# Where attention's sums are divided by their denominators

## The chip, the cores and the metric

The kernel runs on one core of a Trainium2 chip. The metric is the device time of one launch in microseconds, as the median of several runs; before the change it is 3389.54 us over 3 runs. Engines are named as in the profile: PE is TensorE, DVE is VectorE, ACT is ScalarE, POOL is GpSimd, and SP is the queue that issues the DMAs.

## The reference

Two layers of graph attention and one transformer layer work on 4096 rows of 256 features, all under the same 4096 x 4096 mask. Only the transformer layer is touched by the change:

```
qkv = layer_norm(x, g1, be1) @ w_qkv            # 8 heads of 32
scores = einsum('nhd,mhd->hnm', q, k) * SCALE
attn = softmax(where(mask, scores, -inf))
out = einsum('hnm,mhd->nhd', attn, v).reshape(n, 256)
x = x + out @ w_proj + b_proj
ff = gelu(layer_norm(x, g2, be2) @ w1 + b1) @ w2 + b2
return x + ff
```

The softmax is computed as exponentials without a shift, then sums of values (numerators) and sums of weights (denominators), and one multiplication by the inverse denominator per row and head.

## The kernel before

The transformer layer is `unshifted_transformer`. It has three parts: queries, keys and values; attention; and a last stage with the output projection, a layer norm and the two matmuls of the feed-forward part. Rows are taken in 8 blocks (`nb`) of 512. The 256 features are two groups (`c`) of 128, each holding four heads, so that attention consists of 16 such quads of heads, `(nb, c)`, with 32 tiles of 128 keys (`mt`) in each. A unit is one `(nb, c, mt)`; there are 512.

For every unit PE computes the scores of four heads in two halves (L1652), ACT takes the exponentials in place in PSUM (L1659), and DVE multiplies by the mask and writes `u_e` to SBUF (L1661). PE adds values weighted by `u_e` to `u_av` (L1666, from `weigh`). For the denominators, POOL adds the `u_e` of two neighbouring units (`u_both`, L1749), and PE multiplies these sums by ones and accumulates `u_dn` (L1666, from `total`), so that POOL has two additions for every pair of units. `u_e` has 10 buffers, `u_both` 6, scores 3 and each of the two sums one bank of PSUM. The order of PE, ACT and DVE in attention is that of the program text (`manual_schedule`); that of POOL and SP, and that of all engines in the last stage, is a planner's, which puts an instruction where it expects it to be ready.

At the end of a quad, ACT copies the numerators from PSUM to `u_num` (L1682, two buffers) and the denominators to `u_den` (L1697). The denominators' way to their inverse goes through DRAM. Four DMAs store one row per head to `den_d` (L1699). Then a list of later steps, `later`, gives one step after every second unit: `step_load` loads them as 128 x 16 (L1702), `step_invert` takes the reciprocal on DVE and stores it to `inv_d` (L1706, L1707), `step_spread` loads it with each head's row repeated over 32 partitions into `u_wide` by four DMAs (L1712), and `step_out` multiplies `u_num` by `u_wide` on DVE (L1720) and stores the product to `att_d` in DRAM (L1721). The steps of the last quad run after the last unit.

The last stage starts with `rows_of(0)`, which loads the residual rows `u_xres` (L742 in the profile) and `u_att`, 128 x 2 x 512, from `att_d` (L1786), each with two buffers. `projected` adds the bias to the residual rows on POOL (L1793), multiplies `u_att` by `w_proj` on PE (L1797), adds the product to the residual rows on DVE (L1804), takes mean, squares and root (L1375, L1383, L1390), normalises (L1401, L1403), and adds the next bias on POOL (L1807). Then PE transposes the normalised rows (L1416), multiplies by `w1` (L1833), ACT takes the gelu (L1840), PE multiplies by `w2` (L1849), DVE adds (L1856) and the rows go out in four DMAs (L1857). The loop over blocks has the loads and `projected` of block `nb + 1` in front of block `nb`'s feed-forward part:

```
for nb in range(NNB):
    more = nb + 1 < NNB
    if more:
        res_next, res_n = projected(*rows_of(nb + 1))
...
    if more:
        hn = turned(res_n)
...
```

Of the kernel before, what the change touches and what calls it, by code (L numbers as in the profile page):

```python
# [8 lines left out]
F32 = mybir.dt.float32  # L9
# [8 lines left out]
ALU = mybir.AluOpType  # L18
# [4 lines left out]
P = 128  # L23
# [694 lines left out]
def spread(src, ap):  # L718

    return bass.AP(tensor=src.tensor, offset=src.offset, ap=ap)  # L720
# [765 lines left out]
def unshifted_transformer(  # L1486
# [22 lines left out]
    nc = tc.nc  # L1509
    N, D = out.shape  # L1510
    DC = D // P
# [3 lines left out]
    NB = 512  # L1515
# [3 lines left out]
    HC = 4  # L1519
    O = P // HC  # L1520
# [7 lines left out]
    inv_d = dram.tile([NQ, HC, NB], F32, name="inv_d")  # L1528
    att_d = dram.tile([DC, P, N], F32, name="att_d")
# [7 lines left out]
    with ExitStack() as scope:  # L1537
# [31 lines left out]
        with ExitStack() as qkv:  # L1569
# [8 lines left out]
            for nb in range(NNB):  # L1578
                cols = slice(nb * NB, (nb + 1) * NB)
# [43 lines left out]
                for b in (nb - 1,) if nb + 1 < NNB else (nb - 1, nb):  # L1623
                    if b >= 0:
                        at = slice(b * NB, (b + 1) * NB)
# [11 lines left out]
        tail = scope.enter_context(tc.tile_pool(name="u_tail", bufs=1))  # L1637
        ps_s = scope.enter_context(tc.tile_pool(name="u_ps_s", bufs=3, space=PSUM))
        ps_a = scope.enter_context(tc.tile_pool(name="u_ps_a", bufs=1, space=PSUM))
        sums_of = {}  # L1640
        later = []
# [32 lines left out]
        def weigh(nb, c, mt, es):  # L1674
            if mt == 0:
                sums_of["av"] = ps_a.tile([P, NB], F32, name="u_av")
            h = c * HC
            lefts = [v_sb[:, mt, (h + j) * O : (h + j + 1) * O] for j in range(HC)]
            four(sums_of["av"], lefts, es, mt == 0, mt == NT - 1)
            if mt == NT - 1:  # L1680
                num = tail.tile([P, NB], F32, name="u_num", bufs=2)
                nc.scalar.copy(num, sums_of["av"])  # L1682
                sums_of[nb, c] = num

        def total(nb, c, mt, both):

# [5 lines left out]

        def quad_end(nb, c):
            at = nb * DC + c
            cols = slice(nb * NB, (nb + 1) * NB)
            den = tail.tile([P, NB], F32, name="u_den")
            nc.scalar.copy(den, sums_of["dn"])  # L1697
            for j in range(HC):
                nc.sync.dma_start(den_d[at, j : j + 1, :], den[j * O : j * O + 1, :])  # L1699

            def step_load():
                nc.sync.dma_start(dens[:, at, :], spread(den_d[at], [[QI, P], [1, QI]]))  # L1702

            def step_invert():
                inv = tail.tile([P, QI], F32, name="u_inv")
                nc.vector.reciprocal(inv, dens[:, at, :])  # L1706
                nc.sync.dma_start(spread(inv_d[at], [[QI, P], [1, QI]]), inv)  # L1707

            def step_spread():
                wide = tail.tile([P, NB], F32, name="u_wide")  # L1710
                for j in range(HC):
                    nc.sync.dma_start(  # L1712
                        wide[j * O : (j + 1) * O, :],
                        spread(inv_d[at, j : j + 1, :], [[0, O], [1, NB]]),
                    )
                sums_of["wide"] = wide

            def step_out():
                num = sums_of.pop((nb, c))
                nc.vector.tensor_tensor(num, num, sums_of["wide"], op=ALU.mult)  # L1720
                nc.sync.dma_start(att_d[c, :, cols], num)  # L1721

            later.extend([step_load, step_invert, step_spread, step_out])

# [6 lines left out]
        for i in range(len(units) + 5):  # L1733
            if i < len(units):
                nb, c, mt = units[i]
# [23 lines left out]
    with ExitStack() as scope:  # L1759
        big = scope.enter_context(tc.tile_pool(name="u_big", bufs=1))  # L1760
        ln = scope.enter_context(tc.tile_pool(name="u_ln2", bufs=2))
        tail = scope.enter_context(tc.tile_pool(name="u_ff", bufs=2))
        ps_m = scope.enter_context(tc.tile_pool(name="u_ps_m", bufs=8, space=PSUM))
        wp_sb = big.tile([P, DC, D], F32, name="u_wp")
        nc.sync.dma_start(wp_sb, w_proj.rearrange("(c p) e -> p c e", p=P))

        def by_row(src, name):
            t = big.tile([P, D], F32, name=name)
            nc.sync.dma_start(t, spread(src, [[0, P], [1, D]]))
            return t.unsqueeze(1).to_broadcast([P, TB, D])  # L1770

        bp_sb = by_row(b_proj, "u_bp")
        wp_sb = big.tile([P, DC, D], F32, name="u_wp")
        nc.sync.dma_start(wp_sb, w_proj.rearrange("(c p) e -> p c e", p=P))


        inside = big.tile(list(dens.shape), F32, name="u_inside")
        nc.vector.tensor_scalar(inside, dens, DEN_MIN, DEN_MAX, op0=ALU.max, op1=ALU.min)
        nc.vector.tensor_tensor(inside, inside, dens, op=ALU.is_equal)
        nc.vector.tensor_reduce(checks.column(), inside, AX.XY, ALU.min)  # L1780

        def rows_of(nb):
            res = tail.tile([P, TB, D], F32, name="u_xres")
            rows.load(res, nb * TB)
            att = tail.tile([P, DC, NB], F32, name="u_att")
            nc.sync.dma_start(  # L1786
                att, att_d[:, :, nb * NB : (nb + 1) * NB].rearrange("c p n -> p c n")
            )
            return res, att

        def projected(res, att):

            nc.gpsimd.tensor_tensor(res, res, bp_sb, op=ALU.add)  # L1793
            for t in range(TB):
                pp = ps_m.tile([P, NB], F32, name="misc")
                for k in range(DC):
                    nc.tensor.matmul(  # L1797
                        pp[:, :D],
                        att[:, k, t * P : (t + 1) * P],
                        wp_sb[:, k, :],  # L1800
                        start=(k == 0),
                        stop=(k == DC - 1),
                    )
                nc.vector.tensor_tensor(res[:, t, :], res[:, t, :], pp[:, :D], op=ALU.add)  # L1804
            res_n = ln.tile([P, TB, D], F32, name="ln_rows")
            norms.normed(res_n, res, *norms.moments(res, ln.tile([P, D], F32, name="ln_square")))
            nc.gpsimd.tensor_tensor(res, res, b2_sb, op=ALU.add)  # L1807
            return res, res_n


        first = rows_of(0)
        b2_sb = by_row(b2, "u_b2")
        w1_sb = big.tile([P, DC, F], F32, name="u_w1")
        nc.sync.dma_start(w1_sb, w1.rearrange("(c p) f -> p c f", p=P))
        w2_sb = big.tile([P, FC, D], F32, name="u_w2")
        nc.sync.dma_start(w2_sb, w2.rearrange("(c p) e -> p c e", p=P))
        def turned(res_n):
            hn = ln.tile([P, DC, NB], F32, name="ln_cols")
            for c in range(DC):
                norms.turned(hn, c, res_n, ps_m.tile([P, NB], F32, name="misc"), 2)  # L1820
            return hn

        res, res_n = projected(*first)
# [5 lines that stand above are left out]
            hid = tail.tile([P, FC, NB], F32, name="u_hid")  # L1829
            for f in range(FC):  # L1830
                ph = ps_m.tile([P, NB], F32, name="misc")
                for k in range(DC):
                    nc.tensor.matmul(  # L1833
                        ph,
                        w1_sb[:, k, f * P : (f + 1) * P],
                        hn[:, k, :],
                        start=(k == 0),
                        stop=(k == DC - 1),
                    )
                nc.scalar.activation(  # L1840
                    hid[:, f, :], ph, AF.Gelu_apprx_tanh, bias=norms.sb["b1"][:, f : f + 1]
                )
            if more:
                hn = turned(res_n)
            for t in range(TB):
                at = t * P
                po = ps_m.tile([P, NB], F32, name="misc")
                for f in range(FC):
                    nc.tensor.matmul(  # L1849
                        po[:, :D],  # L1850
                        hid[:, f, at : at + P],
                        w2_sb[:, f, :],
                        start=(f == 0),
                        stop=(f == FC - 1),
                    )
                nc.vector.tensor_tensor(res[:, t, :], res[:, t, :], po[:, :D], op=ALU.add)  # L1856
                nc.sync.dma_start(  # L1857
                    out[nb * NB + at : nb * NB + at + P, :], res[:, t, :]
                )
            if more:  # L1860
                res = res_next
# [110 lines left out]
```

## Time and profile before

| | |
|---|---|
| median of the runs | 3389.54 us (3386.7 to 3389.91, 3 runs) |
| the profiled execution | 3386.81 us; its span 3385.0 us |
| granted PE clock, mean | 0.982 |
| busy, share of the span | PE 93%, DVE 86%, ACT 78%, POOL 39% |
| 1930 to 3040 us, within attention: busy of 1110 us | DVE 1095.06, POOL 1071.65, PE 1046.26, ACT 917.19 |
| 3110 to 3385 us, last stage: busy of 275 us | PE 258.92, ACT 91.62, DVE 48.67, POOL 35.26 |
| first and last `u_both` start | 1850.3 and 3091.1 us |
| L1720, `u_num` times `u_wide`, 16 times | 691 to 3671 ns, median 3251 |
| L1712, loads of `u_wide`, 64 DMAs of 64 KB | 415 ns of SP each (median) |

The span is the time from the first to the last record of one profiled execution; the launch takes a little longer, and the median of the runs differs a little from this one execution. Busy times count an instruction from its start to its end as the profiler sees them, with any waiting in between. Attention runs from about 1850 to 3094 us, the last stage from there to the end.

### The profile page before, as it was taken

The page shows a single profiled execution, that of the slowest core. Times are in us where ns is not written, and L with a number is a line of the kernel's source. Part 1 is how long each engine was busy: PE and PEld are TensorE (multiplying, and loading weights), DVE is VectorE, ACT ScalarE, POOL GpSimd, SP SyncE. Part 2 cuts the span into 40 slices and gives each one's busy share as a digit, 9 for nine tenths or more (in the row PEclk, how much of TensorE's full clock was granted, in tenths as well). Part 3 has the DMA queues.
Part 4 walks back from the last instruction along what each step waited for, and adds up shares of the span by engine and source line. Part 5 has one row for each costly group of instructions (what it writes and reads, how often), then busy time and mean ns, then how long its engine had stood idle before and what let it go on. Part 6 is the DMA issues. An engine that isn't in the chain of part 4 may idle for free.

```text
span 3385.0 us, 109959 instructions
## 1 busy us (share of the span) xinstructions
PE 3161.2 (93%) x49300; PEld 2316.7 (68%) x49300; DVE 2897.8 (86%) x3242; ACT 2638.5 (78%) x3417; POOL 1326.4 (39%) x600
## 2 busy tenths in 40 slices
PE   4899999999889999999988999999999999997998
PEld 3799999999879999999965433333333333333666
DVE  5899999999889989999975999999999999996111
ACT  4799899898768888888875887888888888875332
POOL 2300000000220000000000999999999999996110
PEclk8999999999999999999999999999999999998999
DMA  6656545531211212111126010101010110002110
GB/s 209 204 180 207 155 152 170 146 91 32 80 56 34 90 52 71 40 59 59 28 73 180 2 49 18 39 21 33 21 32 27 26 45 12 28 11 79 42 45 27
DMA packets 210706, 247.44 MB, mean 73 GB/s; under 512 B 88304, under 2 KB 131568, under 8 KB 210224
## 3 DMA queue, kind: packets, MB, share of 16 engines
q1 hardware_dynamic: 210224, 240.31, 23.7%
q8 instruction: 388, 6.36, 0.8%
q14 instruction: 94, 0.77, 0.1%
HBM read 197.80 MB, written 42.47 MB: 71 GB/s over the span
## 4 chain that ended last, share of the span: by engine, by line
DVE 23%; PE 13%; POOL 7%; issue 5%; ACT 4%; DMA 1%; SPq 0%; DVEq 0%; POOLq 0%; ACTq 0%
DVE u_e L1661 20%; POOL u_both L1749 7%; PE misc L1849 3%; PE bank L1330 2%; PE u_ps L1652 2%; PE misc L1595 2%; PE u_av L1666 2%; ACT u_ps L1659 1%; ACT t L1078 1%; PE misc L1833 1%; PE u_dn L1666 1%; PE misc L1614 1%; PE misc L1416 1%; DVE t L1085 1%; DMA u_xres<-rows 1%
## 5 line engine op out<-in xcount | busy, mean ns | idle before, releaser
L1330 PE MATMUL bank<-vst,t 128*128 128x66 f16 (+1 forms) x24576 | 1523.4, 203 | 53.2 <-DVE t L1085 46.0
L1330 PEld LDWEIGHTS <-t 128*128 128x128 fp8e4 x24576 | 1504.9, 97 | 74.3 <-DVE t L1085 55.7
L1749 POOL TENSOR_TENSOR u_both<-u_e 128x1024 f32<-128x1024 f32 x512 | 1198.1, 2389 | 884.6 <-DMA u_k<-half_d 839.6
L1330 PE MATMUL bank<-vst,mask 128*128 128x132 f16 x8192 | 1505.0, 222 | 1.8 <-issue 1.8
L1078 ACT ACTIVATE t<-s_b,g_terms 128x1024 int8<-128x1024 f32 x1151 | 1248.9, 1173 | 100.7 <-PE bank L1330 93.1
L1661 DVE SCALAR_TENSOR_TENSOR u_e<-u_mask,u_ps 128x1024 f32<-128x1024 uint8 x1024 | 1171.0, 1212 | 15.8 <-ACT u_ps L1659 13.8
L1659 ACT ACTIVATE u_ps<-u_ps 128x1024 f32<-128x1024 f32 x1024 | 1010.6, 1010 | 219.4 <-PE u_ps L1652 180.9
L1330 PEld LDWEIGHTS <-mask 128*128 128x128 fp8e4 x8192 | 803.3, 98 | 0.0
L1652 PE MATMUL u_ps<-u_q,u_k 128*32 128x512 f16 x8192 | 637.2, 384 | 79.5 <-DVE u_e L1661 64.6
L1652 PEld LDWEIGHTS <-u_k 128*32 128x32 f16 x8192 | 279.0, 96 | 618.7 <-issue 566.2
L1085 DVE TENSOR_TENSOR t<-t,mask 128x2048 int32<-128x2048 int32 x256 | 590.9, 2308 | 107.0 <-ACT t L1078 85.7
L1080 DVE TENSOR_SCALAR t<-s_b,g_terms 128x1024 fp8e4<-128x1024 f32 x897 | 634.7, 750 | 0.0
L1666 PE MATMUL u_av<-u_e,u_v 128*32 128x512 f32 x4096 | 545.0, 602 | 0.1
L1019 POOL TENSOR_TENSOR vst<-g_prod,vst 128x528 f16<-128x528 f32 x32 | 39.0, 1232 | 817.8 <-DVE vst L1018 793.7
L1666 PE MATMUL u_dn<-u_both,u_ones 128*32 128x512 f32 x2048 | 271.9, 597 | 1.7 <-POOL u_both L1749 1.7
L1666 PEld LDWEIGHTS u_av<-u_e,u_v 128*32 128x32 f32 x4096 | 136.7, 110 | 95.5 <-issue 3.1
L1840 ACT ACTIVATE u_hid<-misc,n_b 128x512 f32<-128x512 f32 x64 | 42.4, 685 | 142.0 <-PE misc L1833 141.9
L1856 DVE TENSOR_TENSOR u_xres<-u_xres,misc 128x256 f32<-128x256 f32 x32 | 13.5, 421 | 122.7 <-PE misc L1849 122.7
L1849 PE MATMUL misc<-u_w,u_hid 128*128 128x256 f32 x512 | 111.8, 379 | 0.0
L1833 PE MATMUL misc<-ln_cols,u_w 128*128 128x512 f32 x256 | 111.2, 592 | 0.0
L1336 ACT COPY ev_broad<-bank 128x396 f32<-128x396 f32 x192 | 89.7, 476 | 22.4 <-PE bank L1330 19.1
L1849 PEld LDWEIGHTS misc<-u_w,u_hid 128*128 128x128 f32 x512 | 96.7, 190 | 13.3 <-issue 0.5
(145 smaller groups left out, 1656.1 us busy)
## 6 DMA issues: line engine op xcount, KB each, us to landing
g_adj<-in_adj_dram SPq DMA_DIRECT2D x123, 512.0 KB
mask<-mask SPq DMA_DIRECT2D x128, 256.0 KB
s_b<-s_d SPq DMA_DIRECT2D x64, 512.0 KB
u_mask<-mask SPq DMA_DIRECT2D x32, 512.0 KB
mask<-stage SPq DMA_DIRECT2D x48, 256.0 KB
rows<-e_x SPq DMA_DIRECT2D x32, 256.0 KB
half_d<-u_halves SPq DMA_DIRECT2D x32, 256.0 KB
u_q<-half_d SPq DMA_DIRECT2D x32, 256.0 KB
```

Of the source, the lines that this page charges most:

```text
L1078: nc.scalar.activation(to.bitcast(I8), s, AF.Sign, bias=negd, scale=-1.0)
L1080: nc.vector.tensor_scalar(to, s, negd, None, op0=ALU.is_ge, saturate=False)
L1085: nc.vector.tensor_tensor(both, both, m32.unsqueeze(1).to_broadcast(list(both.shape)), op=ALU.bitwise_and)
L1330: nc.tensor.matmul(to, left, right, start=k not in opened, stop=last)
L1336: nc.scalar.copy(ev[0][:, a:b].rearrange("p s v -> p (s v)"), acc[k][:, : (b - a) * 2 * VW],)
L1652: nc.tensor.matmul(ps[r * O : (r + 1) * O, j, :], k_st[:, h, at : at + O], q_st[:, h, :], start=True, stop=True,)
L1659: nc.scalar.activation(ps, ps, AF.Exp, scale=SCALE)
L1661: nc.vector.scalar_tensor_tensor(e, mask, 0.0, ps, op0=ALU.not_equal, op1=ALU.mult)
L1666: nc.tensor.matmul(to[j * O : (j + 1) * O, :], lefts[j], es[j // 2][:, j % 2, :], start=start, stop=stop,)
L1749: nc.gpsimd.tensor_tensor(both, es_of[i - 1][u], es_of[i][u], op=ALU.add)
L1833: nc.tensor.matmul(ph, w1_sb[:, k, f * P : (f + 1) * P], hn[:, k, :], start=(k == 0), stop=(k == DC - 1),)
L1849: nc.tensor.matmul(po[:, :D], hid[:, f, at : at + P], w2_sb[:, f, :], start=(f == 0), stop=(f == FC - 1),)
```

## The change

The numerators leave attention as they are: `weigh` stores `u_num` to `att_d` right after ACT's copy. `quad_end` keeps the steps that load and invert the denominators and store `inv_d`; `step_spread` and `step_out` are gone. In the last stage `rows_of` also loads the inverse denominators of a block, both groups of four heads in one tile `u_wide` of 128 x 2 x 512 with two buffers, by four DMAs, and `projected` multiplies `u_att` by it on DVE before the projection's matmuls.

```diff
@@ weigh
                 num = tail.tile([P, NB], F32, name="u_num", bufs=2)
                 nc.scalar.copy(num, sums_of["av"])
-                sums_of[nb, c] = num
+                nc.sync.dma_start(att_d[c, :, nb * NB : (nb + 1) * NB], num)
@@ quad_end
-            def step_spread():
-                wide = tail.tile([P, NB], F32, name="u_wide")
-                for j in range(HC):
-                    nc.sync.dma_start(
-                        wide[j * O : (j + 1) * O, :],
-                        spread(inv_d[at, j : j + 1, :], [[0, O], [1, NB]]),
-                    )
-                sums_of["wide"] = wide
-
-            def step_out():
-                num = sums_of.pop((nb, c))
-                nc.vector.tensor_tensor(num, num, sums_of["wide"], op=ALU.mult)
-                nc.sync.dma_start(att_d[c, :, cols], num)
-
-            later.extend([step_load, step_invert, step_spread, step_out])
+            later.extend([step_load, step_invert])
@@ rows_of, projected
-            return res, att
-
-        def projected(res, att):
+            inv = tail.tile([P, DC, NB], F32, name="u_wide")
+            for j in range(HC):
+                nc.sync.dma_start(
+                    inv[j * O : (j + 1) * O],
+                    spread(inv_d[nb * DC, j : j + 1, :], [[0, O], [HC * NB, DC], [1, NB]]),
+                )
+            return res, att, inv
+
+        def projected(res, att, inv):
 
             nc.gpsimd.tensor_tensor(res, res, bp_sb, op=ALU.add)
+            nc.vector.tensor_tensor(att, att, inv, op=ALU.mult)
```

## The prediction

> **What bounds the kernel now.** I read the page's groups first, because the change takes one VectorE (DVE) multiplication out of each of the 16 groups of four heads ("quads") of attention. Columns: line, engine, operation, output and inputs, count, then busy us and mean ns of one, then the idle time before it.
>
> ```profile
> L1749 POOL TENSOR_TENSOR u_both<-u_e 128x1024 f32<-128x1024 f32 x512 | 1198.1, 2389 | 884.6 <-DMA u_k<-half_d 839.6
> ...
> L1661 DVE SCALAR_TENSOR_TENSOR u_e<-u_mask,u_ps 128x1024 f32<-128x1024 uint8 x1024 | 1171.0, 1212 | 15.8 <-ACT u_ps L1659 13.8
> L1659 ACT ACTIVATE u_ps<-u_ps 128x1024 f32<-128x1024 f32 x1024 | 1010.6, 1010 | 219.4 <-PE u_ps L1652 180.9
> ```
>
> Attention has 256 pairs of key tiles. A pair is 4 exponentials, 4 maskings and 2 GpSimd (POOL) additions. Next come the instructions of the multiplication's line, with minimum/median/maximum in ns, and the DVE timeline around one of them (start, us, engine, line).
>
> ```profile
> L1720 DVE TENSOR_TENSOR u_num<-u_num,u_wide x16: 691/3251/3671, 1953.0 to 3111.0; 128x512 f32<-128x512 f32 x16
> ...
> 2176.59 9.13 DVE L1661 SCALAR_TENSOR_TENSOR u_e<-u_mask,u_ps 128x1024 f32<-128x1024 uint8 x8
> 2185.64 3.29 DVE L1720 TENSOR_TENSOR u_num<-u_num,u_wide 128x512 f32<-128x512 f32 x1
> 2188.85 5.81 DVE L1661 SCALAR_TENSOR_TENSOR u_e<-u_mask,u_ps 128x1024 f32<-128x1024 uint8 x5
> 2195.85 58.47 DVE L1661 SCALAR_TENSOR_TENSOR u_e<-u_mask,u_ps 128x1024 f32<-128x1024 uint8 x51 [1.18 <-ACT u_ps L1659]
> ```
>
> The same instruction takes 691 ns after attention has ended and about 3250 within it. DVE looks 98.7% busy (1095 of 1110 us from 1930 to 3040), but some 2.5 us of each multiplication are waiting that is counted as busy. So I don't take DVE for the bound, and look at POOL's timeline (brackets: idle before).
>
> ```profile
> 2113.64 74.74 POOL L1749 TENSOR_TENSOR u_both<-u_e 128x1024 f32<-128x1024 f32 x32 [1.76 <-DVE u_e L1661]
> 2190.14 9.38 POOL L1749 TENSOR_TENSOR u_both<-u_e 128x1024 f32<-128x1024 f32 x4 [1.76 <-DVE u_e L1661]
> 2200.79 65.33 POOL L1749 TENSOR_TENSOR u_both<-u_e 128x1024 f32<-128x1024 f32 x28 [1.26 <-DVE u_e L1661]
> ```
>
> POOL runs without a break except after each multiplication: 1.76 us at once, and in 10 of 15 cases 1.26 to 1.49 us more some 12 us later. The view by stage explains the second gap (columns: stretch, length, busy us and count of PE, PEld, DVE, ACT, POOL, granted clock, DMA share, GB/s).
>
> ```profile
> 1879.00:1953.00 74.00, 72.71 (x912) 30.63 (x911) 73.94 (x66) 64.70 (x68) 74.00 (x33) 1.00 0.05 13
> 1953.00:1965.00 12.00, 8.50 (x92) 3.00 (x88) 10.76 (x9) 5.86 (x6) 10.21 (x6) 0.86 0.07 24
> ```
>
> While DVE waits, TensorE (PE) starves, its clock falls, and ACT, DVE and POOL in turn lack work. In the stretch before the first multiplication (the first of the two lines) the clock is whole and POOL is busy for all of 74 us. **POOL is the bound, interrupted by the multiplications.**
>
> **What the Trainium skill says.** "SBUF — State Buffer", Who interferes with whom: a DVE instruction with two SBUF inputs fully blocks against a GpSimd instruction that reads SBUF, while one with at most one SBUF input doesn't contend. The trace agrees: 3251 against 691 ns for L1720 (two SBUF inputs), while u_e, with only the mask in SBUF, keeps its pace beside a busy POOL. "VectorE: DVE Perf Modes", The TRN2 errata: an fp32 tensor_tensor takes (N+151)/0.96 ns; for N=512 that is 691, just the trace's minimum. "Perfetto Trace Analysis", GPSIMD Engine Instruction: time these by start-to-start spacing. Here 28 additions in 65.33 us with the last at 2.389 give (65.33-2.389)/27 = 2.331 us; the mean of 2.389 would be too long. "TensorE: Matmul & The Clock Gate", What's actually happening: the clock is halved after an idle window of about 3.4 us. The trace shows 0.86 over those 12 us, or 1.7 us of clock lost, which is 3.4 us at half.
>
> **The change part by part.**
>
> *Attention, DVE.* 15 multiplications leave, 3.05 to 3.67 us each, 49.3 us in sum (the 16th ran after the last tile). But POOL sets the pace: 2 x 2.331 = 4.66 us a pair, against DVE's 4 x 1.144 = 4.58 (56 maskings in 64.15 us) and ACT's 4 x 1.01 = 4.04. PE's pair, at full clock, lasts 4.53 in the trace with some waiting in it. So not 49 but POOL's idle time is gained: 15 x 1.76 = 26.4, and the ten second gaps, 13.6: **-40.0 us**. Check: a quad lasts (3037.65-1953.04)/14 = 77.47 us now; 32 x 2.331 = 74.6 at POOL's pace; 15 x 2.9 = 43. Next late is POOL's addition; DVE then waits for PE, which waits for POOL's sum. Lower bound of the gain: the first gaps alone, 26; upper: 43.
>
> *Attention, SP.* Per quad 4 loads of u_wide (0.415 us of issue each) leave; the store of att_d moves up some 26 us, to the copy on ACT. SP waits there for ACT and might hold what is queued behind: den_d's stores, which wait for a copy 5 us later anyway, and the mask and query loads of the next block, asked for most of a quad ahead. Nothing, as long as that lead stands; without it, up to those 5 us per quad. No instruction is added to POOL, PE or ACT; num's two buffers come free sooner.
>
> *The start of the last stage.* The first projection waited for u_att; now it waits for four u_wide loads and a multiplication too. Lines of the timelines of SP, PE and DVE:
>
> ```profile
> 3096.90 0.47 SPq L1786 DMA_DIRECT2D u_att<-att_d  x1
> 3101.08 6.00 PE L1797 MATMUL misc<-u_wp,u_att 128*128 128x256 f32 x16 [6.54 <-DMA u_att<-att_d]
> 3107.39 1.72 SPq L1712 DMA_DIRECT2D u_wide<-inv_d  x4
> 3109.15 0.42 SPq L742 DMA_DIRECT2D u_xres<-rows  x1
> ...
> 3113.45 3.39 DVE L1403 TENSOR_SCALAR ln_rows<-u_xres,n_mean,n_dev 128x256 f32<-128x256 f32 x4
> ```
>
> Four issues last 1.7 us, so the last load lands about that much behind u_att; the multiplication of 128x1024 isn't in the trace: (1024+151)/0.96 = 1.22 us by the page above, and 0.42 at 256 and 0.69 at 512 extend to the same. Together +2.9; bounds +1.2 (loads issued early) and +5 (behind POOL's addition of 2.35 too). Against it, SP no longer stands before the last quad's u_wide loads (3107.39) until inv_d has landed, so u_xres of block 1 comes before 3109.15, and POOL's addition for it no longer meets ln_rows, four instructions that last 3.39 us there and 1.38 in later blocks: -1.5. Bounds 0 and -2. Sum **+1.4 us**.
>
> *Each later block.* 4 more DMAs of 128 KB and 1.22 us of DVE. PE is the bound here, 32.8 of 33 us. The loads reach two blocks ahead (u_att at 3154.18 serves the projection at 3217), so neither transfers nor the wait of PE for att matter. SP's four issues, 1.7 us, fit between its waits. What has no slack is the chain u_xres - POOL L1793 - DVE L1804 - norm - transposes (timelines again):
>
> ```profile
> 3152.96 0.38 SPq L742 DMA_DIRECT2D u_xres<-rows  x1
> 3154.18 0.38 SPq L1786 DMA_DIRECT2D u_att<-att_d  x1
> 3157.72 2.35 POOL L1793 TENSOR_TENSOR u_xres<-u_xres,u_bp 128x1024 f32<-128x1024 f32 x1 [22.10 <-DMA u_xres<-rows]
> 3168.76 1.73 PE L1416 MATMUL misc<-ident,ln_rows 128*128 128x128 f32 x8 [0.88 <-DVE ln_rows L1403]
> ```
>
> PE already waits 0.2 to 0.9 us for it. u_att lands near 3158.5, while POOL's addition reads SBUF until 3160.07; a multiplication placed there waits for it and then runs 1.22 us ahead of L1804, so the block grows by 1.2. If DVE's order puts it after the mean (ends 3162.98; DVE then idles 5.1 us) it costs nothing. Lower bound 0, upper 3.6 (its own time and an addition of 2.35) for each of 7 blocks, 25. It concerns the four blocks whose u_att arrives there (4.8 us); at even odds **+2.4 us**.
>
> *Sum:* -40.0 + 1.4 + 2.4 = -36.2. The profiled execution took 3386.81 us (span 3385.0 and 1.8 around it): 3350.6. It stands 2.7 us below the median of the runs, 3389.54; I forecast the median: **3353 us**.
>
> **Rivals.** *The second gaps stay* (waits on POOL's sums let PE idle enough to lose its clock): 3389.5 - 26.4 + 3.8 = 3367. Against it: POOL's unbroken runs show a clock of 1.00. *The multiplications meet POOL's additions in every block*: 25 instead of 2.4, 3376. For it: u_att's landing beside L1793; against it: 5 us of idle DVE just after. *Slower:* one block's loads lose their lead. If SP places u_wide behind the block's output stores, or DVE's order sets the multiplication behind the previous block's last additions (L1856), then load (4 us for u_att, 3 for u_wide by that rate) and multiplication stand before each projection: up to 7 x 11 = 77 us, 3389.5 - 38.6 + 77 = 3428. It decides from 38.6/7 = 5.5 us a block. Against it: double buffers, and u_wide's buffer is free as soon as its multiplication ends, a block earlier than u_att's. *No effect:* the stall would stay if something else in the DVE queue took POOL's ports; the reciprocal, 0.24 us with one input, is all that's left there.
>
> **How the numbers follow.** Forecast 0.74, second gaps 0.08, additions met 0.10, slower 0.06, no effect 0.02. The range takes in a larger gain (43, no start cost, PE waits gone: 3342) and reaches to 3372, between the two slower-paced cases. 0.2% of 3389.5 is 6.8 us, about what a measurement of this kernel can tell from no change; the first three cases are all faster by more: 0.92, within 0.02, slower 0.06.
>
> **What would show it.** POOL's timeline: one run of over 500 additions at 2.33 us without gaps of 1.76; a clock near 1.00 through attention; POOL's last u_both some 40 us earlier; DVE with more idle time than before although it does less. In the last stage: L1797's first matmul 2 to 4 us after u_att's landing, and PE's idle time before L1416 at 0.2 to 2 us. The forecast is wrong if POOL runs gapless and the additions' spacing grows, if the gaps stay without a multiplication, or if PE waits over 5 us a block before L1797.

## The result and the profile after

| | before | after |
|---|---|---|
| median of 6 runs each | 3388.43 us (3386.7 to 3389.91) | 3357.95 us (3356.51 to 3359.76) |
| profiled execution, span | 3386.81, 3385.0 us | 3358.87, 3357.1 us |
| granted PE clock, mean | 0.982 | 0.985 |

The ratio is 0.9911, 95% interval [0.9899, 0.9923]: 30.5 us less by the medians, 27.9 between the two profiled executions. The change is under 1%, but the slowest run after is 27 us below the fastest before. The forecast was 3353 us in a range of 3342 to 3372.

The page's group of POOL's additions has nearly the same mean as before (2384 ns against 2389) and nearly the same busy time (1198.3 us against 1198.1). Its line number has moved with the edit.

```profile
L1734 POOL TENSOR_TENSOR u_both<-u_e 128x1024 f32<-128x1024 f32 x512 | 1198.3, 2384 | 842.7 <-DVE u_e L1661 842.7
```

What changed is when they run. POOL's timeline after (start, us, engine, line; in brackets the idle time before):

```profile
1860.65 6.68 POOL L1734 TENSOR_TENSOR u_both<-u_e 128x1024 f32<-128x1024 f32 x2 [3.55 <-DVE u_e L1661]
1868.72 1185.88 POOL L1734 TENSOR_TENSOR u_both<-u_e 128x1024 f32<-128x1024 f32 x508 [1.38 <-DVE u_e L1661]
3056.28 2.34 POOL L1784 TENSOR_TENSOR u_xres<-u_xres,u_bp 128x1024 f32<-128x1024 f32 x1 [1.68 <-issue]
```

All the gaps that had followed the multiplications are gone: after the first four additions come 508 in one run, 1185.88/508 = 2.334 us each. The view by stage (stretch, length, busy us and count of PE, PEld, DVE, ACT, POOL, clock, DMA share, GB/s) has PE's clock whole; in the kernel before it was 0.86 in the shorter stretch, which held a multiplication there:

```profile
1930.00:3040.00 1110.00, 1106.06 (x13336) 555.42 (x13331) 1098.47 (x969) 939.82 (x984) 1110.00 (x476) 1.00 0.09 24
1953.00:1965.00 12.00, 11.86 (x156) 5.01 (x151) 12.00 (x12) 10.47 (x12) 12.00 (x6) 1.00 0.00 1
```

PE and DVE are recorded as busy nearly all the time too, so this view alone can't tell which of the three is the bound; the experiments below do.

The span divides at three places: POOL's first `u_both`, the end of its last one, and the first matmul with `w1` (L1833 before, L1825 after).

| | before | after | difference |
|---|---|---|---|
| to the first `u_both` | 1850.28 | 1851.41 | +1.1 |
| first to end of last `u_both` | 1243.14 | 1203.19 | -39.95 |
| from there to the first projection matmul | 7.66 | 14.04 | +6.4 |
| from there to the first matmul with `w1` | 21.03 | 22.14 | +1.1 |
| from there to the end | 262.89 | 266.32 | +3.4 |
| span | 3385.0 | 3357.1 | -27.9 |

The first row has nothing of the change in it. Attention gives 40 us, and the last stage takes 10.9 back. SP's timeline at its start shows where most of that comes from:

```profile
3058.75 0.47 SPq L1771 DMA_DIRECT2D u_att<-att_d  x1
3059.39 0.34 SPq L1701 DMA_DIRECT2D u_dens<-den_d  x1
3059.78 0.90 SPq L1776 DMA_DIRECT2D u_wide<-inv_d  x2
3063.45 0.34 SPq L1706 DMA_DIRECT2D inv_d<-u_inv  x1
3063.84 0.90 SPq L1776 DMA_DIRECT2D u_wide<-inv_d  x2
3064.78 0.42 SPq L1754 DMA_DIRECT2D u_b<-in_L_gnn_b_dram  x1
```

SP takes up its instructions one after the other. Two of block 0's four loads of `u_wide` stand behind the last quad's `inv_d` store, which waits for a reciprocal, which waits until the denominators have been loaded (3059.39 to 3063.1). So SP stands still for 2.8 us, though block 0's inverses have been in DRAM for a millisecond. On DVE and then PE:

```profile
3067.32 1.22 DVE L1785 TENSOR_TENSOR u_att<-u_att,u_wide 128x1024 f32<-128x1024 f32 x1 [2.58 <-DMA u_wide<-inv_d]
```

```profile
3068.64 5.29 PE L1789 MATMUL misc<-u_wp,u_att 128*128 128x256 f32 x16 [12.19 <-DVE u_att L1785]
3080.95 2.19 PE L1416 MATMUL misc<-ident,ln_rows 128*128 128x128 f32 x8 [7.02 <-DVE ln_rows L1403]
3085.57 5.37 PE L1789 MATMUL misc<-u_wp,u_att 128*128 128x256 f32 x16 [2.43 <-DVE u_att L1785]
...
3138.01 1.62 PE L1416 MATMUL misc<-ident,ln_rows 128*128 128x128 f32 x8 [1.46 <-DVE ln_rows L1403]
```

PE waits 12.19 us for block 0's product, where it had waited 6.54 for `u_att` alone, and another 2.43 for block 1's, and it waits 1.46 us before the transposes in a later block, where it had been 0.88. DVE's timeline of that block shows why:

```profile
3128.20 1.41 DVE L1796 TENSOR_TENSOR u_xres<-u_xres,misc 128x256 f32<-128x256 f32 x4 [8.38 <-POOL u_xres L1784]
3129.53 1.22 DVE L1785 TENSOR_TENSOR u_att<-u_att,u_wide 128x1024 f32<-128x1024 f32 x1
3130.67 1.21 DVE L1375 TENSOR_REDUCE n_mean<-u_xres 128x4 f32<-128x1024 f32 x1
```

The multiplication for a later block stands between the residual additions and the mean, and delays the norm by 1.14 us.

### The profile page after: what moved, and what is told of

Same layout as the page of the kernel before. It is cut to its first block, busy times and chain, and to the rows that moved or that the text cites. A ratio compares the mean times of both kernels' runs of the same rounds, so it can differ in the third digit from the quotient of the medians.

```text
span 3357.1 us, 109908 instructions
## 1 busy us (share of the span) xinstructions
PE 3184.6 (95%) x49300; PEld 2421.7 (72%) x49300; DVE 2867.5 (85%) x3234; ACT 2625.8 (78%) x3417; POOL 1327.2 (40%) x600
## 3 DMA queue, kind: packets, MB, share of 16 engines
q1 hardware_dynamic: 209712, 240.31, 23.8%
## 4 chain that ended last, share of the span: by engine, by line
PE 37%; DVE 9%; ACT 3%; DMA 2%; issue 2%; POOL 0%; SPq 0%; DVEq 0%; POOLq 0%; ACTq 0%
PE u_av L1666 11%; PE u_ps L1652 10%; PE u_dn L1666 6%; DVE u_e L1661 6%; PE misc L1841 3%; PE bank L1330 3%; PE misc L1595 2%; ACT u_ps L1659 1%; PE misc L1825 1%; DMA u_xres<-rows 1%; PE misc L1614 1%; ACT t L1078 1%; DVE t L1085 1%; PE misc L1416 1%; POOL u_xres L1784 0%
## 5 line engine op out<-in xcount | busy, mean ns | idle before, releaser
L1734 POOL TENSOR_TENSOR u_both<-u_e 128x1024 f32<-128x1024 f32 x512 | 1198.3, 2384 | 842.7 <-DVE u_e L1661 842.7
L1661 DVE SCALAR_TENSOR_TENSOR u_e<-u_mask,u_ps 128x1024 f32<-128x1024 uint8 x1024 | 1179.5, 1214 | 12.5 <-ACT u_ps L1659 1.2
L1659 ACT ACTIVATE u_ps<-u_ps 128x1024 f32<-128x1024 f32 x1024 | 998.0, 1008 | 189.1 <-PE u_ps L1652 146.1
L1652 PE MATMUL u_ps<-u_q,u_k 128*32 128x512 f16 x8192 | 720.8, 381 | 15.3 <-DVE u_e L1661 10.6
L1652 PEld LDWEIGHTS <-u_k 128*32 128x32 f16 x8192 | 344.3, 96 | 441.5 <-issue 332.3
L1666 PE MATMUL u_av<-u_e,u_v 128*32 128x512 f32 x4096 | 586.0, 594 | 0.1
L1666 PE MATMUL u_dn<-u_both,u_ones 128*32 128x512 f32 x2048 | 319.4, 598 | 3.4 <-POOL u_both L1734 3.4
L1666 PEld LDWEIGHTS u_av<-u_e,u_v 128*32 128x32 f32 x4096 | 166.4, 110 | 107.8 <-DVE u_e L1661 1.6
L1666 PEld LDWEIGHTS u_dn<-u_both,u_ones 128*32 128x32 f32 x2048 | 97.0, 109 | 71.7 <-POOL u_both L1734 6.1
L1825 PE MATMUL misc<-ln_cols,u_w 128*128 128x512 f32 x256 | 111.2, 592 | 0.0
```

The costliest lines, as they stand in the source:

```text
L1652: nc.tensor.matmul(ps[r * O : (r + 1) * O, j, :], k_st[:, h, at : at + O], q_st[:, h, :], start=True, stop=True,)
L1659: nc.scalar.activation(ps, ps, AF.Exp, scale=SCALE)
L1661: nc.vector.scalar_tensor_tensor(e, mask, 0.0, ps, op0=ALU.not_equal, op1=ALU.mult)
L1666: nc.tensor.matmul(to[j * O : (j + 1) * O, :], lefts[j], es[j // 2][:, j % 2, :], start=start, stop=stop,)
L1734: nc.gpsimd.tensor_tensor(both, es_of[i - 1][u], es_of[i][u], op=ALU.add)
L1825: nc.tensor.matmul(ph, w1_sb[:, k, f * P : (f + 1) * P], hn[:, k, :], start=(k == 0), stop=(k == DC - 1),)
```

## The experiments

e1 to e4 ran on one chip together with the kernel before, at 3387.3 us there; e5 to e8 on another one, with the kernel before at 3387.24. Ratios are to the kernel before on the same chip, with a 95% interval.

### What is it in the removed multiplication that cost time?

`e2_two_inputs` puts one tiny product of two SBUF slices in the place of the old multiplication (one more line, not shown, keeps `num` for it):

```diff
-            later.extend([step_load, step_invert])
+            num = sums_of.pop((nb, c))
+
+            def step_extra():
+                side = tail.tile([P, QI], F32, name="u_side")
+                nc.vector.tensor_tensor(side, num[:, :QI], num[:, QI : 2 * QI], op=ALU.mult)
+
+            later.extend([step_load, step_invert, lambda: None, step_extra])
```

> The changed kernel with one more DVE instruction per quad at the old place of the multiplication: a product of two 128x16 slices in SBUF, about 0.17 us of work, whose result isn't used. Theory A (two SBUF inputs wait for POOL's ports, however small the work): each lasts some 2.5 us, POOL's gaps of more than 1 us after each of the 15 come back, with dips of PE's clock; 3380 to 3395 us. Theory B (what counts is DVE's time at work): 15 x 0.17 = 2.6 us, 3358 to 3361.

Measured: 3384.78 us, ratio 0.9991 [0.9984, 0.9997] to the kernel before. Its instructions (minimum/median/maximum ns), and POOL's timeline:

```profile
L1713 DVE TENSOR_TENSOR u_side<-u_num x16: 111/2774/3274, 1955.3 to 3092.9; 128x16 f32<-128x16 f32 x16
```

```profile
2113.10 74.74 POOL L1741 TENSOR_TENSOR u_both<-u_e 128x1024 f32<-128x1024 f32 x32 [1.25 <-DVE u_e L1661]
2189.08 9.40 POOL L1741 TENSOR_TENSOR u_both<-u_e 128x1024 f32<-128x1024 f32 x4 [1.24 <-DVE u_e L1661]
2199.88 65.39 POOL L1741 TENSOR_TENSOR u_both<-u_e 128x1024 f32<-128x1024 f32 x28 [1.40 <-DVE u_e L1661]
```

Work of 0.11 us (the one that ran after attention) takes 2774 ns beside POOL. The gaps are back: 15 of 1.24 us and seven second ones of 1.26 to 1.50, 28.6 us in sum, and POOL's additions take 1232.2 us from first to last, 29.0 more than after the change. Each product, here as in the kernel before, begins by its record during one addition on POOL, doesn't get in when that addition ends and the next one begins, and ends just after that next one: by 0.03 to 0.04 us here, by 0.55 for the 128x512 of before, in all 15 cases of each. By then POOL has nothing left to add, and goes on 1.2 us after the product, when DVE has written the next `u_e`. So of the 1.76 us of a first gap, 0.52 went with the size of the product and 1.24 with the waiting alone.

The time comes so close to the kernel before because this kernel also has the scaling in the last stage: its attention is 11 us faster than that of the kernel before (1232.2 against 1243.1), and its last stage some 10 us slower.

Around the stalls at 1955 and 2185 us, which have a second gap, PE's clock is 0.89 over 16 us; around that at 2263, which has none, it is 1.00. The kernel before has the same division, here at the stalls of 2031 and 2109 us (columns as above, with the clock behind POOL's count):

```profile
2031.00:2045.00 14.00, 10.92 (x119) 3.95 (x112) 12.51 (x10) 8.01 (x10) 12.24 (x6) 0.88 0.05 20
2109.00:2118.00 9.00, 5.95 (x76) 2.43 (x72) 9.00 (x7) 5.04 (x6) 7.24 (x4) 1.00 0.08 31
```

It is so for all 30 stalls of the two kernels: the 17 with a fall of the clock are the 17 with a second gap.

`e3_one_input` has a sum over `u_num` at the same place, with one SBUF input (the rest of the edit is that of e2):

```diff
+                nc.vector.tensor_reduce(side[:, 0:1], num, AX.X, ALU.add)
```

> The changed kernel with one more DVE instruction per quad at the same place: a sum over the 512 columns of u_num, one SBUF input, as much work as the old multiplication (about 0.69 us), result unused. Theory A (POOL is the bound and one SBUF input doesn't wait): each lasts 0.6 to 0.75 us, POOL's run of additions stays whole; 3357 to 3360 us. Theory B (DVE is the bound): 15 x 0.69 = 10 us more, 3368.

Measured: 3356.07 us, 0.9903 [0.9888, 0.9919]. Instruction, and POOL's timeline:

```profile
L1713 DVE TENSOR_REDUCE u_side<-u_num x16: 627/678/680, 1954.2 to 3062.2; 128x1 f32<-128x512 f32 x16
```

```profile
1868.71 1185.19 POOL L1741 TENSOR_TENSOR u_both<-u_e 128x1024 f32<-128x1024 f32 x508 [1.38 <-DVE u_e L1661]
```

Six times the work of e2 costs nothing: it takes its 0.68 us at once, and POOL runs on. DVE has room, so DVE isn't the bound. e2 and e3 differ in the operation too, a product and a sum; no run has both forms of one operation. That e2's product alone took 0.11 us, and that each one's end follows the end of an addition on POOL, speaks for the inputs.

`e7_before_on_pool` is the kernel before with one word changed:

```diff
-                nc.vector.tensor_tensor(num, num, sums_of["wide"], op=ALU.mult)
+                nc.gpsimd.tensor_tensor(num, num, sums_of["wide"], op=ALU.mult)
```

> The kernel before, with the multiplication of u_num by u_wide on POOL instead of DVE, nothing else. Theory A (POOL is the bound of attention; DVE's waits cost POOL 40 us, and 15 multiplications of 128x512 at about 1.2 us on POOL cost 18): no gap of 1.76 us is left, attention's additions take some 22 us less than before; 3362 to 3369 us. Theory B (DVE is the bound and 49 us of its time are freed): 3338 to 3347.

Measured: 3365.53 us, 0.9937 [0.9923, 0.995]. POOL's timeline:

```profile
2107.41 1.42 POOL L1720 TENSOR_TENSOR u_num<-u_num,u_wide 128x512 f32<-128x512 f32 x1
2108.66 74.86 POOL L1749 TENSOR_TENSOR u_both<-u_e 128x1024 f32<-128x1024 f32 x32
2183.33 1.42 POOL L1720 TENSOR_TENSOR u_num<-u_num,u_wide 128x512 f32<-128x512 f32 x1
```

No gap is left, and each multiplication takes 1.25 us from start to start (2107.41 to 2108.66). From the first to the last addition are 1221.4 us: the 1203.2 of the changed kernel and 15 x 1.25 = 18.8 give 1222. What is put on POOL is paid in full, what is put on DVE (e3) isn't. POOL is the bound of attention once the stalls are gone, although PE and DVE look almost as busy.

### What does the last stage's part cost, and why?

`e1_unscaled` leaves this part out:

```diff
-            inv = tail.tile([P, DC, NB], F32, name="u_wide")
-            for j in range(HC):
...
-            nc.vector.tensor_tensor(att, att, inv, op=ALU.mult)
```

> The changed kernel without the four loads of u_wide per block and without the multiplication in the last stage; the output is left unscaled. It prices the last stage's part of the change by itself. Theory A (attention gives back some 39 us, and the part in the last stage costs some 11: 7.5 at its start and 3.4 in the later blocks): 3345 to 3350 us, POOL's run of additions as in the changed kernel, PE's wait before the transposes (L1416) back at 0.2 to 0.9 us a block. Theory B (attention gives only some 30 and the last stage costs nothing): 3357 to 3359.

Measured: 3346.6 us, 0.9878 [0.9863, 0.9893]. PE's timeline:

```profile
3060.38 6.57 PE L1782 MATMUL misc<-u_wp,u_att 128*128 128x256 f32 x16 [6.39 <-DMA u_att<-att_d]
3073.79 2.19 PE L1416 MATMUL misc<-ident,ln_rows 128*128 128x128 f32 x8 [6.84 <-DVE ln_rows L1403]
3075.77 5.65 PE L1782 MATMUL misc<-u_wp,u_att 128*128 128x256 f32 x16
...
3127.46 1.73 PE L1416 MATMUL misc<-ident,ln_rows 128*128 128x128 f32 x8 [0.43 <-DVE ln_rows L1403]
```

POOL's last addition ends at 3052.24; the projection starts 8.1 us later instead of 14.0, the first matmul with `w1` 29.0 instead of 36.2, and from there to the end are 263.2 us instead of 266.3. So the part costs 7.2 at the start and 3.1 afterwards.

`e4_first_loads_act` lets another queue issue block 0's `u_wide`:

```diff
-                nc.sync.dma_start(
+                (nc.scalar if nb == 0 else nc.sync).dma_start(
                     inv[j * O : (j + 1) * O],
```

> The changed kernel with block 0's four loads of u_wide issued from ACT instead of SP. Theory A (the start of the last stage is late because two of these loads stand in SP behind the last quad's inv_d store, which waits for a reciprocal): the first projection's matmuls start 9.5 to 12 us after POOL's last addition instead of 14.0; 3354 to 3356 us. Theory B (their transfer and the multiplication themselves take that long): 14 us again, 3357 to 3359.

Measured: 3356.57 us, 0.9905 [0.989, 0.9921], just above the 3354 to 3356 expected. The ratio's interval doesn't part it from the changed kernel's, so the traces have to. PE's timeline:

```profile
3065.30 5.62 PE L1789 MATMUL misc<-u_wp,u_att 128*128 128x256 f32 x16 [8.50 <-DVE u_att L1785]
...
3083.21 5.22 PE L1789 MATMUL misc<-u_wp,u_att 128*128 128x256 f32 x16 [2.43 <-DVE u_att L1785]
```

POOL ended at 3055.14, so the first projection starts 10.2 us after it instead of 14.0, and the first matmul with `w1` 33.1 instead of 36.2. The queue's order was the larger part of what the first wait had grown by, 3.9 of 6.4 us. Block 1's wait of 2.43 us stays: its loads stand behind 2 MB of weights.

`e5_mult_after_mean` changes only DVE's order:

```diff
-            nc.vector.tensor_tensor(att, att, inv, op=ALU.mult)
+            with tc.issue_after(norms.last.ins) if ahead_of else ExitStack():
+                nc.vector.tensor_tensor(att, att, inv, op=ALU.mult)
```

Here `norms.last` is the second instruction of the mean of the block before, L1376.

> The changed kernel with one edge of order on DVE: the multiplication of a block is issued after the mean of the block before it (L1376) instead of ahead of it. Theory A (it stands in the chain that PE's transposes wait for, at 1.14 us in each of four blocks): PE's wait before L1416 falls from 1.3 to 1.5 us to 0.2 to 0.6 in those blocks, and the time by 2.5 to 4 us against the changed kernel run beside it. Theory B (PE's wait comes from the loads, not from this place): no difference beyond 1 us.

Measured: 3354.02 us, 0.9902 [0.9887, 0.9917], against 3357.28 of the changed kernel beside it (`e8_changed_again`): 3.3 us less, as expected, but the runs of the two overlap (up to 3356.36 here, from 3355.48 there), so the traces count for more. DVE's timeline, then PE's:

```profile
3129.18 1.42 DVE L1797 TENSOR_TENSOR u_xres<-u_xres,misc 128x256 f32<-128x256 f32 x4 [8.33 <-POOL u_xres L1784]
3130.63 1.22 DVE L1375 TENSOR_REDUCE n_mean<-u_xres 128x4 f32<-128x1024 f32 x1
3131.89 0.17 DVE L1376 TENSOR_SCALAR n_mean<-n_mean 128x4 f32<-128x4 f32 x1
3131.97 1.22 DVE L1786 TENSOR_TENSOR u_att<-u_att,u_wide 128x1024 f32<-128x1024 f32 x1
```

```profile
3137.84 1.73 PE L1416 MATMUL misc<-ident,ln_rows 128*128 128x128 f32 x8 [0.26 <-DVE ln_rows L1403]
```

PE waits 0.26, 0.53, 0.24 and 0.21 us in the four blocks instead of 1.46, 1.40, 1.35 and 1.29 (1.57, 1.78, 1.25 and 1.39 in e8), and from the first matmul with `w1` to the end are 262.8 us, as before the change. The start was late in this run, 38.9 us after POOL's end against 36.2 and 34.1 in the two profiles of the changed kernel, so part of it isn't seen in the profiled time.

`e8_changed_again` is the changed kernel itself, for that comparison.

> The changed kernel itself, beside the three others, so that they are compared with it on one chip: 3355 to 3360 us.

Measured: 3357.28 us, 0.9913 [0.9897, 0.9928]. In its profile the first projection starts 13.35 us after POOL's end, and PE doesn't wait for block 1's product. The first matmul with `w1` is earlier than in the first profile, 34.1 us instead of 36.2, and from there to the end it takes longer, 268.3 instead of 266.3:

```profile
3169.70 1.63 PE L1416 MATMUL misc<-ident,ln_rows 128*128 128x128 f32 x8 [1.78 <-DVE ln_rows L1403]
3171.17 15.67 PE L1841 MATMUL misc<-u_w,u_hid 128*128 128x256 f32 x64
```

The 64 matmuls last 1.7 us longer than the 13.98 of other blocks: after that wait the clock fell once more. The whole of the last stage, from POOL's end, is 302.5 us in both profiles and 291.6 before the change, so the price of 10.9 is firm, but its division differs from run to run by some 2 us.

`e6_start_and_order` puts it together: the orders of e4 and e5, and the loads of blocks 0 and 1 ahead of the others, with `w_proj` loaded once where it was loaded twice.

```diff
+        first = rows_of(0)
+        wp_sb = big.tile([P, DC, D], F32, name="u_wp")
...
+        bp_sb = by_row(b_proj, "u_bp")
+        second = rows_of(1)
...
-                res_next, res_n = projected(*rows_of(nb + 1))
+                res_next, res_n = projected(*(rows_of(nb + 1) if nb else second))
```

> The changed kernel with the order of e5_mult_after_mean, block 0's u_wide from ACT, the loads of blocks 0 and 1 ahead of the other loads of the last stage, and one load of w_proj instead of two. Theory A (the start of the last stage is late because its loads stand in SP's queue behind the last quad's stores and 2 MB of weights): the first projection starts 6 to 10 us after POOL's last addition instead of 14.0, L1825 starts 25 to 29 us after it instead of 36.2, PE doesn't wait before block 1's projection; 9 to 14 us below the changed kernel, some 3344 to 3349 us. Theory B (transfers and the chain of the norm set the start): within 5 us of the changed kernel.

Measured: **3344.77 us**, 0.9875 [0.986, 0.989], 12.5 us below the changed kernel beside it and 42.5 below the kernel before. PE's timeline:

```profile
3060.45 5.13 PE L1790 MATMUL misc<-u_wp,u_att 128*128 128x256 f32 x16 [5.41 <-DVE u_att L1786]
3075.22 2.19 PE L1416 MATMUL misc<-ident,ln_rows 128*128 128x128 f32 x8 [9.64 <-DVE ln_rows L1403]
3077.20 5.22 PE L1790 MATMUL misc<-u_wp,u_att 128*128 128x256 f32 x16
```

POOL ended at 3053.06: 7.4 us to the projection (7.7 in the kernel before), 29.2 to the first matmul with `w1`, and 262.3 from there to the end. With its loads and its place in order, the last stage is as short as without the scaling: 291.4 us from POOL's end, against 292.3 in e1. That doesn't make the scaling itself free, as e6 also moves the other loads and has one load of `w_proj` less, and no run has these without the scaling. The first matmul with `w1` misses the expectation of 25 to 29 slightly. POOL's first addition of the bias starts 9.1 us after its last `u_both`, against 1.7 in the changed kernel, and the norm follows that; `b_proj` is issued after the denominators' stores in e6 and before them in the changed kernel, which is the likely cause, but no run tries it.

## Why the prediction was right

**Attention, -40.0: right, and for its reason.** Measured -39.95. POOL's timeline became the one run that was named, the clock went to 1.00, and e2 and e3 part the wait for POOL from the work on DVE, as the Trainium skill ("SBUF — State Buffer", Who interferes with whom) has it: two SBUF inputs contend with a GpSimd instruction that reads SBUF, one (outside the two-port modes) doesn't (2774 against 678 ns here). The choice that carried the number was to sum POOL's idle time and not the 49.3 us of the multiplications: those would have forecast 9 us too much. That PE's clock makes the second gap is what the stages show (ten second gaps in the kernel before, and ten falls of the clock within attention, at the same stalls); no run holds the clock fixed, so this link isn't tested by itself. The prediction explained the fall by an idle window of about 3.4 us. The 3.4 us are the length of the fall in the trace, but PE was idle for at most 2.99 us at a time, so an idle time of that length wasn't needed.

**One sign of it was wrong.** DVE was to show more idle time. It has 11.5 us of 1110 (1098.47 busy), against 14.9 before. The maskings that fit into the time gained fill the record, and busy time isn't room: e3's 0.68 us fitted nonetheless.

**The start of the last stage, +1.4: the term that was mis-sized.** It measured +7.5 in the first profile and +5.4 in the second (e8). Before the first projection it is +6.4 and +5.7, where +2.9 was put and +5 was the upper bound. The step assumed four issues in a row behind `u_att`. The step's own view showed what breaks them up: SP waiting for the last quad's chain of denominators. I had seen SP held by that chain in the kernel before (the `u_wide` loads at 3107.39), counted the release as a gain, and not asked what would stand behind the chain's remaining store. e4 takes 3.9 of the first wait away by the queue alone. The multiplication's 1.22 us was right (1218 ns in the median), so what was mis-sized is the wait for the loads. The sign named for it was missed as well: the first matmul starts some 5.9 us after `u_att` has landed and not 2 to 4, if the load takes the 4.0 us that it took before.

The relief of 1.5 came, but not as described. The normalisation that had met POOL's addition is as short as in later blocks, or nearly:

```profile
3080.30 1.57 DVE L1403 TENSOR_SCALAR ln_rows<-u_xres,n_mean,n_dev 128x256 f32<-128x256 f32 x4
```

That is 1.8 us less than the 3.39 before, though POOL's addition for block 1 starts later after the last `u_both`, 23.8 us instead of 20.0: its load is issued earlier, as forecast, but right behind 2 MB of weights. The normalisation itself starts later still, at 3080.30, when that addition is nearly over (3080.75). In the first profile the relief was then lost to PE's wait of 2.43 us for block 1's product, a wait that the sum had put at nothing.

**The later blocks, +2.4: 3.4, and 5.4 in the second profile.** Mechanism and count of blocks were right, and e5 shows it: four blocks, about 1 us each. The rest of the 5.4 is mostly the fall of the clock shown with e8, a cost that the term didn't have. I had left it at even odds whether DVE's order would put the multiplication ahead of the mean or behind it; it came between the residual additions and the mean, where it didn't wait for POOL.

**The rivals.** The second gaps didn't stay. The multiplications met no POOL addition for long: their maximum is 1727 ns against a median of 1218. Lost lead, the slower case, is what happened to blocks 0 and 1 alone, 14.6 us of PE's waiting for their products in the first profile, of which 6.5 had been there for `u_att` before; in the later blocks loads kept their lead, and no later projection waited for its product. SP's earlier store of `att_d` cost attention nothing: POOL's run has no break.

**Luck.** The median is 5 us above the forecast, the profiled execution 8.3 above the 3350.6 worked out for it: 7 from the two terms of the last stage and 1.1 from ahead of attention, which the change doesn't touch. That the median came nearer is the doing of the 2.7 us added for it: the profile after lies 0.9 above its median, not below. And the number of second gaps, 13.6 of the 40 us, is that of the one profile of the kernel before; e2, with shorter stalls, had seven.

## What to carry to other kernels

Where DVE and GpSimd both work, look at the shortest and the longest instance of the same DVE instruction before its busy time is believed: 691 and 3251 ns of one shape say that it waits, and then its gain is what the waiting does to the bound engine, not its own duration. When a step is moved into another stage, walk down the issuing queue at the new place and ask of every entry ahead of it what it waits for; loads whose data have long been ready belong ahead of a store at the end of a chain, or on another queue. A multiplication that nobody waits for can still sit in a chain by its engine's order, and one edge of order removes that.

## What the runs showed of the hardware that was not expected

- A product that waits for POOL waits for more than the addition in progress, however small its own work: 128x16 took 2774 ns in the median where 128x512 took 3251; the medians differ by 477 ns, the shortest instances (691 and 111 ns) by 580. The waiting, some 2.6 us, is the same for both, and longer than one addition on POOL (2.33 us): in none of the 30 cases did the product get in between two additions that followed each other.
- PE's clock fell although PE was never idle for the 3.4 us that the fall lasts: idle times of 2.1 to 3.0 us, with another of 0.5 just after, were enough in 17 of the 30 stalls, and one of 1.78 in e8's last stage. The falls start on a fixed grid of 3.413 us (the ten in the kernel before are whole multiples of it apart), and which stalls lose the clock goes with their place on that grid more than with their length: PE resumed 0.42 to 0.75 of a step after a grid point in the 17 stalls that lost the clock, and 0.10 to 0.40 in the 13 that kept it.
- An SP instruction that issues a DMA, 0.3 to 0.5 us as a rule, took up to 3.38 us in the changed kernel (`u_att` at 3068.06), while the loads of 2 MB of weights and of block 1 were under way; e8 has 3.49 us at the same place. The issue itself was then part of the delay. That the transfers under way are the reason isn't tested by itself.
